# One set of PSUM banks for scores, turned probabilities and results in the soft-disc layer of a four-layer network, with four banks left to the side work, and an early start for that layer

## The chip, the cores and the metric

The program runs on one core of one Trainium2 chip, in one launch. The metric is the device time of an execution in microseconds (us). Everything is computed in fp32. A core has a matrix engine (TensorE, PE in the profile), a vector engine (VectorE, DVE), a scalar engine for functions such as Exp and Tanh (ScalarE, ACT), a general engine (GpSimd, POOL) and a queue that issues transfers (SyncE, SP). Matrix products land in PSUM, which the kernel uses as eight banks of 512 fp32 columns on 128 partitions. Each engine runs its instructions in the order in which they were written.

## The reference

The input has 8 images of 32x32 positions and 256 channels. Four layers follow each other, each of the form `x = x + f(groupnorm(x))`. Layer 0 is a retention layer, layer 1 a gated recurrent layer in its parallel form, layer 2 a 7x7 neighbourhood attention. The change touches layer 3, an attention with a soft disc as its window, 8 heads of 32 channels, cut here to what matters:

```python
qkv = silu(x @ w_qkv.T)                       # q, k, v
q, k = rms_norm(q, w_qn), rms_norm(k, w_kn)   # within each head
wp = silu(x @ w_wp.T + b_wp)                  # a width and a sharpness per head and position
...
k_win, v_win = unfold2d(k), unfold2d(v)       # 7 x 7 windows around each position
scores = einsum('blhd,blwhd->blhw', q, k_win) * D ** -0.5
soft_mask = sigmoid((width - rel_dist) * sharp)
attn = softmax(scores - (1 - soft_mask) * 10000)
out = einsum('blhw,blwhd->blhd', attn, v_win)
out = rms_norm(out, w_on)
return silu((out + v) @ w_out.T)
```

## The kernel before, in words

The layers run one after the other, and each hands its result to the next through device memory. `K.next` lets the last steps of a layer prepare the first image of the next one: a `First` object loads it, takes its statistics, loads the weights and normalises.

Layer 3 (`layer3`, class `DiscStream`) goes over the images in chunks. A chunk is one image and one half of the channels, that is four heads, so there are 16 chunks. In a chunk there are eight groups of 128 query positions (two 8x8 blocks) whose keys lie in 14x14 windows, 196 keys each. The main loop has a step `n` for each of the 128 groups, and each step works on several groups at once, at different stages:

- `scores(n + 3)`: 16 small matmuls (L1534) into four PSUM banks `s0` to `s3`, one for each head.
- `exps(n)`: Exp on ACT (L1557).
- `units(n)`: side work that is due (see below).
- `logits(n + 3)`: DVE reads the four score banks and adds the mask (L1547).
- `turn(n - 2, 0)`: four transposes on PE (L1575) put two heads' probabilities into one bank of the ring `m`, and one DVE copy of 112x512 (L1580) takes them to SBUF (`pts`).
- `finish()`: the second halves of the side work, which the units handed back.
- `soft(n + 5)` on ACT (L1963), `divide(n)` on DVE and POOL (L1564, L1565), `units(n + 0.5)`, `turn(n - 2, 1)` for the other two heads, and `finish()` again.
- `values(n - 3)`: 24 matmuls (L1591) into the bank `o`, and two DVE copies of 128x64 (L1599) to `oT`.
- `masked(n + 5)` on POOL (L1970).

The next step begins with its own `scores`. The order inside a step is written out by hand, and `manual_schedule` keeps it for PE, ACT, DVE and POOL. The framework puts in the waits: two engines' accesses to the same buffer wait for each other.

The side work is a list of units, each with a due time counted in steps (`Fillers`). It holds the projections of the next chunk (`project`: q, k and v in two halves each, one bank to a half, L1902; Tanh on ACT, L1887; the `rest` on DVE, L1912 and L1914; squares on POOL, L1922), the disc parameters (`discs`, L1935 to L1954), the root mean squares (`roots`, L1982 to L1998, with two changes of ACT's function table), `head_scale` (L2004, L2008), the values' strips and transposes (`in_strips` L2018, `vturn` L1608 and L1613), the group norm of the next image, and the tail of the image before (`tail_sq`, `tail_scale`, `output` L2050 to L2059). Each unit that uses PE takes a bank from the ring `m` and gives it back when its `rest` has read it.

PSUM in layer 3 is thus four score banks, three ring banks (shared by the units and the `pt` of `turn`) and one bank `o`.

Ahead of step 0 the loop begins at `n = -13`, where only units are due: chunk 0 is projected at -12 and on, the discs at -10, and so on. Before that, the head of `layer3` clears three padded key images (`kp`), the strips and nine probability tiles on POOL (L1830, L1518), and brings in the layer's constants by transfers issued from ACT's queue (L1834 to L1857), some of which DVE and POOL then scale (L1835, L1845 to L1850, L1855).

Of the kernel before, what the change touches and what calls it, by code (L numbers as in the profile page):

```python
# [16 lines left out]
P = 128  # L17
SIDE = 32
L = SIDE * SIDE
C = 256  # L20
# [137 lines left out]
class Base:  # L158
    def __init__(self, nc, pool, images, a):
        self.nc, self.pool, self.images = nc, pool, images  # L160
        idg = pool.tile([P, 2, P], F32, name="idg")
        nc.sync.dma_start(idg, a["k_id"])
        self.ident = idg[:, 0, :]
        self.g8 = idg[:, 1, :]
        self.mhalf = pool.tile([P, 2], F32, name="mhalf")
        nc.vector.memset(self.mhalf, -0.5)
        self.ring = None
        self.next = None

    def big(self, name):  # L170

# [183 lines left out]
class First3(First):  # L355
    def weights(self):

        nc = self.K.nc
        self.w = self.K.big("w3")[:, :, 0 : 768 + P]
        nc.vector.memset(self.w[:, :, 784:], 0.0)  # L360
        nc.sync.dma_start(self.w[:, :, 0:768], self.a["l3_qkv"])
        nc.sync.dma_start(self.w[:, :, 768:784], self.a["l3_wp"])

    def norm(self, c):
        if c == 0:
# [1137 lines left out]
class DiscStream(Stream):  # L1503
# [8 lines left out]
    def __init__(self, K, wk, cp, pp, pairs, n_img, ebufs):  # L1512
        super().__init__(K, wk, pp, pairs, n_img, ebufs)
        self.slots, self.s = 20, {}
        self.tiles = []
        for i in range(ebufs):
            t = cp.tile([P, 4, 2 * self.PART], F32, name=f"e{i}")
            self.nc.gpsimd.memset(t, 0.0)  # L1518
            self.tiles.append(t)

    def tile(self, n):
        return self.tiles[n % self.ebufs]
# [3 lines left out]

    def scores(self, n):
        b, c, t = self.groups[n]
        s = [self.pp.tile([P, HALF], F32, tag=f"s{j}", name=f"s{j}") for j in range(4)]
        q, k = self.q[b, c], self.k[b, c]  # L1530
        for g in range(2):
            for j in range(4):
                ch = slice(32 * j, 32 * j + 32)
                self.nc.tensor.matmul(  # L1534
                    grid(s[j][64 * g : 64 * g + 64, :NWIN], self.ROW),
                    q[ch, 64 * t.block(g) : 64 * t.block(g) + 64],
                    k[ch, t.krs[g] : t.krs[g] + self.ROW, t.kc : t.kc + self.ROW],
                    start=True, stop=True,
                )
        self.s[n] = s  # L1540
# [23 lines left out]
        self.nc.vector.reciprocal(self.su, self.su)  # L1564
        self.nc.gpsimd.tensor_mul(e, e, self.su.unsqueeze(2).to_broadcast([P, 4, NWIN]))  # L1565

    def turn(self, n, i):

        if i == 0:
            self.pts[n] = self.wk.tile([P, 2, HALF], F32, name="pts", bufs=2)  # L1570
        ps = self.ring("pt")
        for j in range(2):
            for k in range(2):
                at = (2 * j + k) * P
                self.nc.tensor.transpose(  # L1575
                    ps[: self.PART, at : at + P],
                    self.tile(n)[:, 2 * i + j, k * self.PART : (k + 1) * self.PART],
                    self.K.ident,
                )
        self.nc.vector.tensor_copy(self.pts[n][: self.PART, i, :], ps[: self.PART, :])  # L1580

    def values(self, n):
        b, c, t = self.groups[n]
        pts = self.pts.pop(n)
        v, at = self.v[b, c], 5 * t.col + t.rows[0]
        o = self.pp.tile([P, HALF], F32, tag="o", name="o")

        for k, q0, o0, w in ((1, 64, 0, P), (0, 0, 64, 64), (2, 192, 0, 64)):
            for j in range(4):
                p0 = (j % 2) * 2 * P + q0  # L1590
                self.nc.tensor.matmul(  # L1591
                    o[32 * j : 32 * j + 32, o0 : o0 + w],
                    v[: self.PART, at + k, 32 * j : 32 * j + 32],
                    pts[: self.PART, j // 2, p0 : p0 + w],
                    start=k == 1, stop=k != 1, skip_group_check=True,
                )
        for g in range(2):
            d = self.o[b, c][:, t.token(g) : t.token(g) + 1]
            self.nc.vector.tensor_copy(  # L1599
                bass.AP(d.tensor, d.offset, [d.ap[0], [SIDE, 8], [1, 8]]),  # L1600
                o[:, 64 - 64 * g : 128 - 64 * g].rearrange("p (i j) -> p i j", j=8),
            )
# [16 lines left out]
def layer2(tc, K, src, dst, n_img, a, first):  # L1619
# [3 lines left out]
    with tc.tile_pool(name="l2c", bufs=1, reuse_waits="tile") as cp, tc.tile_pool(  # L1623
# [132 lines left out]
        with tc.manual_schedule(engines={E.PE, E.Activation, E.DVE, E.Pool}):  # L1756
# [4 lines left out]
                    fill.add(at, lambda b=b: x.update({b: load(K.big("x"), b)}))  # L1761
            if K.next:
                nx, n = K.next, 16 * n_img
                fill.add(n - 22, nx.load)
                for i in range(4):
                    fill.add(n - 17 + i, lambda i=i: nx.stats(i))
                fill.add(n - 12, nx.mean)
                fill.add(n - 11, nx.root)
                fill.add(n - 7, nx.weights)
                for c in range(2):  # L1770
                    fill.add(n - 6 + c, lambda c=c: nx.norm(c))
# [42 lines left out]
def layer3(tc, K, src, dst, n_img, a, first):  # L1814
    nc = tc.nc
    pairs = disc_pairs()
    with tc.tile_pool(name="l3c", bufs=1, reuse_waits="tile") as cp, tc.tile_pool(
# [8 lines left out]
        xq[0], w = first.xq, first.w  # L1826
        kpad = [cp.tile([P, PADW, PADW], F32, name=f"kp{i}") for i in range(3)]
        strips = cp.tile([P, 4, PADW + 2, 14], F32, name="strips")
        for t in kpad + [strips]:
            nc.gpsimd.memset(t, 0.0)  # L1830
        st = DiscStream(K, wk, cp, pp, pairs, n_img, 9)
        K.ring = st.ring
        bwp = cp.tile([P, 16], F32, name="bwp")
        nc.scalar.dma_start(bwp, a["l3_bwp"].partition_broadcast(P))  # L1834
        nc.vector.tensor_scalar(bwp, bwp, 0.5, None, ALU.mult)  # L1835
        sel = cp.tile([P, 64], F32, name="sel3")
        nc.scalar.dma_start(sel, a["k_sel3"])
        spread = cp.tile([P, 2, P], F32, name="spread")
        nc.scalar.dma_start(spread[:, 0], a["k_spread"])
        nc.scalar.dma_start(spread[:, 1], a["k_spread"])  # L1840
        won = cp.tile([P, 2, P], F32, name="won")
        nc.scalar.dma_start(won.rearrange("p a b -> p (a b)"), a["l3_qkn"].partition_broadcast(P))


        nc.vector.tensor_mul(won[:, 0], won[:, 0], won[:, 1])  # L1845
        nc.vector.scalar_tensor_tensor(
            spread[:, 0], won[:, 0], -(32.0**-0.5) / MASK_SCALE, spread[:, 0],
            ALU.mult, ALU.mult,
        )
        nc.vector.memset(won, 0.0)  # L1850
        for h in range(2):
            nc.scalar.dma_start(won[32 * h + 8 : 32 * h + 9], a["l3_on"].unsqueeze(0))
        wo = cp.tile([P, 2, C], F32, name="wo3")
        nc.scalar.dma_start(wo, a["l3_out"])
        nc.gpsimd.tensor_scalar(wo, wo, 0.5, None, ALU.mult)  # L1855
        win = cp.tile([P, 2, NWIN], F32, name="win3")
        nc.scalar.dma_start(win, a["k_win3"])  # L1857
        eps = cp.tile([P, 1], F32, name="eps6")
        nc.vector.memset(eps, 1e-6)

        gn = first.gn

# [209 lines left out]
        def plan_chunk(J):  # L2072

            n, (b, c) = 8 * J, divmod(J, 2)
            for i in range(4):
# [7 lines left out]
        def plan_image(b):  # L2083
            n = 16 * b
            if b:
                fill.add(n - 27.5, lambda: load(b))
                for i in range(4):
                    fill.add(
                        n - 23.5 + i / 2,
                        lambda i=i: gn.stats(b, image_parts(x[b]), i),  # L2090
                    )
                fill.add(n - 21, lambda: gn.mean(b, later))
                fill.add(n - 19, lambda: gn.root(b, later))
                for c in range(2):
                    fill.add(n - 13.5 + c / 2, lambda c=c: normed(b, c))
            for u in range(2):
                fill.add(n - 10 + u / 2, lambda u=u: discs(b, u))
# [12 lines left out]
        for J in range(2 * n_img + 3):  # L2110
            b, c = divmod(J, 2)
            t = b - 2 if c == 0 and b >= 2 else None
            if J < 2 * n_img or t is not None:
# [18 lines left out]
        def finish():  # L2132
            while later:
                later.pop(0)()

        E = mybir.EngineType
        with tc.manual_schedule(engines={E.PE, E.Activation, E.DVE, E.Pool}):
            for n in range(-13, N + 3):
                if 0 <= n + 3 < N:
                    b, c, t = st.groups[n + 3]  # L2140
                    if t is pairs[0]:
# [6 lines left out]
                    st.logits(n + 3)  # L2148
                if 0 <= n - 2 < N:
                    st.turn(n - 2, 0)  # L2150
                finish()
                if 0 <= n + 5 < N:
                    soft(n + 5)
                if 0 <= n < N:
                    st.divide(n)
                units(n + 0.5)
                if 0 <= n - 2 < N:
                    st.turn(n - 2, 1)
                finish()
                if 0 <= n - 3 < N:  # L2160
                    st.values(n - 3)
                if 0 <= n + 5 < N:
                    masked(n + 5)
            for n in range(N + 3, N + 32):
                for h in (0, 0.5):
# [7 lines left out]
def body(tc, a, out, layers=LAYERS):  # L2173
# [7 lines left out]
    with tc.tile_pool(name="base", bufs=1) as bp, tc.tile_pool(name="images", bufs=1) as ip:  # L2181
# [10 lines left out]
        for i, layer in enumerate(layers):  # L2192
            K.next = first.get(i + 1)
            layer(tc, K, x[i], x[i + 1], n_img, a, first.get(i))


# [16 lines left out]
```

## Time and profile before

| | |
|---|---|
| median of 3 runs | 3490.29 us (3487.11 to 3499.76) |
| profiled execution | 3481.33 us, span 3479.5 us, mean granted TensorE clock 0.964 |
| busy share of the span | PE 94%, ACT 64%, DVE 62%, POOL 43% |
| layer 3 in the span | about 2622 to 3480 us |
| PE busy, 2700 to 2800 us | 86.40 of 100 us, granted clock 0.82 |
| PE busy, 3000 to 3100 and 3100 to 3200 us | 93.32 and 93.34 of 100 us, granted clock 0.95 and 0.97 |
| first scores of layer 3 | at 2660 us |

The busy shares cover the whole program, and each layer has limits of its own. For this change the stage is layer 3. The windows of that stage, its waits and the order of instructions in single steps are what is to be read; an engine's share in other layers says nothing on it.

### The profile page before, as it was taken

Reading aid. Unit: us, or ns where it says so; the run is one execution under the profiler, and the core shown is the slowest. Engines: PE = TensorE matmul, PEld = TensorE weight load, DVE = VectorE, ACT = ScalarE, POOL = GpSimd, SP = SyncE. Lnnn points to the kernel's source line nnn. Section 1 sums busy time; section 2 is a strip of 40 time slices with the busy share of each in tenths; the row PEclk is TensorE's granted clock in tenths of the full one; section 3 lists DMA queues with packets and bytes.
Section 4 is the critical chain, followed back from the end, with each engine's and each line's share of the span. In section 5 each row is a group of like instructions: output and inputs, shape, how many; then the busy total and the mean of one; then the engine's idle time right before and its main releaser. Section 6 shows DMA issues by size and latency. Waiting matters only on the chain.

```text
span 3479.5 us, 77392 instructions
## 1 busy us (share of the span) xinstructions
PE 3255.0 (94%) x30760; PEld 1655.6 (48%) x30760; DVE 2172.7 (62%) x5559; ACT 2237.1 (64%) x5022; POOL 1491.2 (43%) x1071
## 2 busy tenths in 40 slices
PE   7999999999998988899999989999998889999998
PEld 3323323323323444677676645555553545555454
DVE  4777677677675664555555545556564667677775
ACT  3667667667675554555555446666675778888885
POOL 4233233232221110345444443333335567777777
PEclk9999999999999998899999999999998889999999
DMA  3000000000003667577777531111111001101001
GB/s 135 13 25 1 25 25 1 25 25 1 25 25 116 236 199 256 162 199 179 203 210 187 136 112 38 38 38 50 50 48 43 2 14 38 32 29 35 26 26 59
DMA packets 139054, 268.44 MB, mean 77 GB/s; under 512 B 9218, under 2 KB 77188, under 8 KB 130372
## 3 DMA queue, kind: packets, MB, share of 16 engines
q1 hardware_dynamic: 131152, 241.90, 23.1%
q10 hardware_dynamic: 7540, 21.60, 1.9%
q8 instruction: 242, 3.96, 0.5%
q14 instruction: 120, 0.98, 0.1%
HBM read 178.27 MB, written 85.20 MB: 76 GB/s over the span
## 4 chain that ended last, share of the span: by engine, by line
PE 68%; ACT 10%; DVE 8%; DMA 5%; POOL 4%; issue 4%; SPq 0%; POOLq 0%; ACTq 0%; DVEq 0%
PE s L633 7%; PE sm L651 6%; PE num L678 5%; PE qkv_ps L1667 5%; PE qkv_ps L1902 4%; PE up_ps L808 3%; PE dn_ps L1205 3%; PE qk_ps L508 3%; DMA x<-x 3%; PE pt L1575 2%; PE pt L1447 2%; PE fac_ps L2004 2%; PE o_ps L561 2%; ACT e L1963 2%; DMA d<-l1rows 2%
## 5 line engine op out<-in xcount | busy, mean ns | idle before, releaser
L639 DVE TENSOR_TENSOR e<-s,ret 128x1024 f32<-128x1024 f32 x512 | 603.0, 1219 | 180.3 <-PE s L633 175.1
L643 ACT ACTIVATE ea<-e 128x1024 f32<-128x1024 f32 x512 | 535.9, 1056 | 267.0 <-DVE e L639 233.4
L633 PE MATMUL s<-qk,qk 32*128 32x512 f32 x2048 | 300.2, 640 | 2.6 <-POOL qk L525 1.9
L1580 DVE COPY pts<-pt 112x512 f32<-112x512 f32 x256 | 176.5, 690 | 181.0 <-PE pt L1575 179.1
L1433 POOL TENSOR_TENSOR e<-e,su 128x616 f32<-128x616 f32 (+2 forms) x128 | 157.4, 1230 | 287.0 <-DVE su L1432 278.8
L1013 POOL TENSOR_TENSOR d<-cmask,d 128x1024 f32<-128x1024 f32 x64 | 152.7, 2386 | 296.0 <-DMA d<-l1rows 183.5
L651 PE MATMUL sm<-ea,ones 128*32 128x512 f32 x2048 | 273.0, 604 | 2.0 <-DVE dn L659 2.0
L678 PE MATMUL num<-e,v 128*32 128x512 f32 x2048 | 266.6, 592 | 0.0
L808 PE MATMUL up_ps<-x,wup 128*128 128x512 f32 x512 | 233.5, 608 | 11.3 <-DVE gate L865 9.3
L1963 ACT ACTIVATE e<-win,disc 128x196 f32<-128x196 f32 x512 | 240.9, 548 | 0.2
L1565 POOL TENSOR_TENSOR e<-e,su 128x784 f32<-128x784 f32 x128 | 191.5, 1496 | 92.3 <-DVE su L1564 67.4
L1557 ACT ACTIVATE e<-e,mx 128x196 f32<-128x196 f32 x512 | 229.1, 456 | 0.0
L1970 POOL TENSOR_TENSOR e<-e,win 128x784 f32<-128x784 f32 x128 | 201.3, 1573 | 38.1 <-issue 32.9
L1667 PE MATMUL qkv_ps<-x,w 128*128 128x512 f32 x384 | 194.7, 644 | 21.3 <-POOL x L239 17.5
L1428 ACT ACTIVATE e<-e,mx 128x154 f32<-128x154 f32 (+2 forms) x512 | 213.4, 429 | 0.2 <-DVE mx L1416 0.2
L1902 PE MATMUL qkv_ps<-xq,w 128*128 128x512 f32 x384 | 199.5, 646 | 11.0 <-DVE kp L1914 5.4
L1575 PEld LDWEIGHTS pt<-idg,e 128*112 128x112 f32 x1024 | 121.1, 141 | 136.9 <-issue 60.1
L1575 PE MATMUL pt<-idg,e 128*112 128x128 f32 x1024 | 167.3, 290 | 19.2 <-DVE pts L1580 8.8
L633 PEld LDWEIGHTS s<-qk,qk 32*128 32x128 f32 x2048 | 85.1, 182 | 184.2 <-issue 121.5
L835 DVE SCALAR_TENSOR_TENSOR cv<-xm,par,cv 128x512 f32<-128x512 f32 x192 | 140.2, 750 | 48.8 <-ACT cv L830 46.2
L1022 ACT ACTIVATE d<-d,cols 128x128 f32<-128x128 f32 x512 | 164.1, 395 | 0.0
L1547 DVE CUSTOM_DVE_ANT_0 e<-s,e 128x196 f32<-128x196 f32 x512 | 154.0, 358 | 12.9 <-PE s L1534 7.8
(241 smaller groups left out, 6644.1 us busy)
## 6 DMA issues: line engine op xcount, KB each, us to landing
d<-l1rows SPq DMA_DIRECT2D x64, 512.0 KB
x<-x SPq DMA_DIRECT2D x25, 1024.0 KB
x<-x SPq DMA_DIRECT2D x32, 512.0 KB
l1xm<-xm SPq DMA_DIRECT2D x16, 1024.0 KB
l1sz<-sz SPq DMA_DIRECT2D x16, 1024.0 KB
xv<-l1xm SPq DMA_DIRECT2D x32, 512.0 KB
l1xa<-xa SPq DMA_DIRECT2D x16, 1024.0 KB
sz<-l1sz SPq DMA_DIRECT2D x16, 1024.0 KB
```

Source lines behind the costliest of these rows:

```text
L633: nc.tensor.matmul(s[:, j % 2], qk[b, 1, c][g, kb * P : (kb + 1) * P], qk[b, 0, c][g, h * HALF : (h + 1) * HALF], start=True, stop=True,)
L639: nc.vector.tensor_mul(e[n, i], s, m)
L643: nc.scalar.activation(ea[n, i], e[n, i], AF.Abs)
L651: nc.tensor.matmul(acc["sm"][g, :], ones, ea[n, j // 2][:, j % 2, :], start=kb == 0, stop=kb == 7,)
L678: nc.tensor.matmul(acc["num"][g, :], v[b][:, kb, vc], e[n, j // 2][:, j % 2, :], start=kb == 0, stop=kb == 7,)
L808: nc.tensor.matmul(ps, wup[:, kc, m * P : (m + 1) * P], seg(s)[:, kc], start=kc == 0, stop=kc == 1,)
L1428: self.nc.scalar.activation(p[:, j], p[:, j], AF.Exp, scale=-1.0, bias=mx[:, j : j + 1], accum_out=su[:, j : j + 1],)
L1557: self.nc.scalar.activation(e[:, j], e[:, j], AF.Exp, scale=-1.0, bias=mx[:, j : j + 1], accum_out=self.su[:, j : j + 1],)
L1575: self.nc.tensor.transpose(ps[: self.PART, at : at + P], self.tile(n)[:, 2 * i + j, k * self.PART : (k + 1) * self.PART], self.K.ident,)
L1667: nc.tensor.matmul(ps, w[:, kc, o : o + P], x[b][:, kc, h * HALF : (h + 1) * HALF], start=kc == 0, stop=kc == 1,)
L1902: nc.tensor.matmul(ps, w[:, kc, o : o + P], xq[b][:, kc, h * HALF : (h + 1) * HALF], start=kc == 0, stop=kc == 1,)
L1963: nc.scalar.activation(e[:, j], win[:, 0], AF.Tanh, scale=disc[b][:, i, 8 + h : 9 + h], bias=disc[b][:, i, h : h + 1],)
```

## The change

It has three parts. First, PSUM: layer 3 now has four tiles `b0` to `b3`, one bank each, cut into two halves of 256 columns. The first half of each takes the scores of one head. The second half of `b0` takes the results `o`; the second halves of `b1`, `b2`, `b3` take the turned probabilities, one head at a time in rotation (`turns`). The ring `m` has four banks, for the units alone. `turn` now handles one head: two transposes and one copy of 112x256, called four times in a step.

Second, the constants: they are loaded and scaled during layer 2 (`First3.early`, three units at steps 88, 92 and 96 of 128), by transfers of the SP queue, into a pool `late` that lives from layer 1 to layer 3.

Third, the first chunk: the loop's steps -13 to -5 are replaced by `start()`, which writes the work of chunk 0 out in an order of its own. Only one padded key image, the strips and three probability tiles are cleared ahead of it, and the others at its end. The statistics of image 1 move to steps -3 and later, and the discs of image 0 go through `start()` alone.

```diff
+    def early(self):
+        nc, a, pool = self.K.nc, self.a, self.K.late
+        def loads():
+            self.bwp = pool.tile([P, 16], F32, name="bwp")
+            nc.sync.dma_start(self.bwp, a["l3_bwp"].partition_broadcast(P))
...
+        def factors():
+            won, spread = self.won, self.spread
+            nc.vector.tensor_scalar(self.bwp, self.bwp, 0.5, None, ALU.mult)
+            nc.gpsimd.tensor_scalar(self.wo, self.wo, 0.5, None, ALU.mult)
...
+        def weight():
+            for h in range(2):
+                nc.sync.dma_start(
+                    self.won[32 * h + 8 : 32 * h + 9], a["l3_on"].unsqueeze(0)
+                )
+        return [loads, factors, weight]
...
+        self.tiles = [cp.tile(shape, F32, name=f"e{i}") for i in range(ebufs)]
+        self.banks = [pp.tile([P, 2, HALF // 2], F32, name=f"b{j}") for j in range(4)]
+        self.turns = 0
+    def ring(self, name):
+        return self.pp.tile([P, HALF], F32, tag="m", name=name, bufs=4)
...
-        s = [self.pp.tile([P, HALF], F32, tag=f"s{j}", name=f"s{j}") for j in range(4)]
+        s = [self.banks[j][:, 0] for j in range(4)]
...
-    def turn(self, n, i):
-        if i == 0:
+    def turn(self, n, j):
+        if j == 0:
             self.pts[n] = self.wk.tile([P, 2, HALF], F32, name="pts", bufs=2)
-        ps = self.ring("pt")
...
-        self.nc.vector.tensor_copy(self.pts[n][: self.PART, i, :], ps[: self.PART, :])
+        ps = self.banks[1 + self.turns % 3][:, 1]
+        self.turns += 1
+        for k in range(2):
+            self.nc.tensor.transpose(
+                ps[: self.PART, k * P : k * P + P],
+                self.tile(n)[:, j, k * self.PART : (k + 1) * self.PART],
+                self.K.ident,
+            )
+        at = (j % 2) * 2 * P
+        self.nc.vector.tensor_copy(
+            self.pts[n][: self.PART, j // 2, at : at + 2 * P], ps[: self.PART]
+        )
     def values(self, n):
...
-        o = self.pp.tile([P, HALF], F32, tag="o", name="o")
+        o = self.banks[0][:, 1]
...
+                for i, u in enumerate(nx.early()):
+                    fill.add(n - 40 + 4 * i, u)
...
-        bwp = cp.tile([P, 16], F32, name="bwp")
-        nc.scalar.dma_start(bwp, a["l3_bwp"].partition_broadcast(P))
...
+        def start():
+            units(-11)
+            rest = [discs(0, 0), discs(0, 1), project(0, 1, 0)]
+            rest[0]()
+            rest[2]()
+            r = project(0, 1, 1)
+            rest[1]()
+            r()
+            soft(0)
+            for h in range(2):
+                project(0, 0, h)()
+            soft(1)
+            rest = [project(0, 2, h) for h in range(2)]
+            for f in rest:
+                f()
+            masked(0)
+            roots(0, None)
+            in_strips(0)
+            for i in range(4):
+                head_scale(0, 1 - i // 2, i % 2)()
+            masked(1)
+            for i in range(3, 9):
+                st.clear(i)
+            for t in kpad[1:]:
+                nc.gpsimd.memset(t, 0.0)
...
-            for n in range(-13, N + 3):
+            start()
+            for n in range(-4, N + 3):
...
                     st.turn(n - 2, 0)
+                    st.turn(n - 2, 1)
...
-                    st.turn(n - 2, 1)
+                    st.turn(n - 2, 2)
+                    st.turn(n - 2, 3)
```

More of the change, by code (lines that the diff above doesn't have):

```diff
@@ L168, in __init__ @@
         self.next = None
+        self.late = pool
     def big(self, name):
@@ L362, in weights @@
         nc.sync.dma_start(self.w[:, :, 768:784], self.a["l3_wp"])
+    def early(self):
[3 more added lines that the diff above has]
+            nc.sync.dma_start(self.bwp, a["l3_bwp"].partition_broadcast(P))
+            self.sel = pool.tile([P, 64], F32, name="sel3")
+            nc.sync.dma_start(self.sel, a["k_sel3"])
+            self.spread = pool.tile([P, 2, P], F32, name="spread")
+            nc.sync.dma_start(self.spread[:, 0], a["k_spread"])
+            nc.sync.dma_start(self.spread[:, 1], a["k_spread"])
+            self.won = pool.tile([P, 2, P], F32, name="won")
+            nc.sync.dma_start(
+                self.won.rearrange("p a b -> p (a b)"), a["l3_qkn"].partition_broadcast(P)
+            )
+            self.wo = pool.tile([P, 2, C], F32, name="wo3")
+            nc.sync.dma_start(self.wo, a["l3_out"])
+            self.win = pool.tile([P, 2, NWIN], F32, name="win3")
+            nc.sync.dma_start(self.win, a["k_win3"])
+            self.eps = pool.tile([P, 1], F32, name="eps6")
+            nc.vector.memset(self.eps, 1e-6)
+        def factors():
+            won, spread = self.won, self.spread
+            nc.vector.tensor_scalar(self.bwp, self.bwp, 0.5, None, ALU.mult)
+            nc.gpsimd.tensor_scalar(self.wo, self.wo, 0.5, None, ALU.mult)
+            nc.vector.tensor_mul(won[:, 0], won[:, 0], won[:, 1])
+            nc.vector.scalar_tensor_tensor(
+                spread[:, 0], won[:, 0], -(32.0**-0.5) / MASK_SCALE, spread[:, 0],
+                ALU.mult, ALU.mult,
+            )
+            nc.vector.memset(won, 0.0)
+        def weight():
+            for h in range(2):
+                nc.sync.dma_start(
+                    self.won[32 * h + 8 : 32 * h + 9], a["l3_on"].unsqueeze(0)
+                )
+        return [loads, factors, weight]
     def norm(self, c):
@@ L1514, in __init__, with clear @@
         self.slots, self.s = 20, {}
[L1515 to L1519, printed above, removed]
+        shape = [P, 4, 2 * self.PART]
+        self.tiles = [cp.tile(shape, F32, name=f"e{i}") for i in range(ebufs)]
[3 more added lines that the diff above has]
+        return self.pp.tile([P, HALF], F32, tag="m", name=name, bufs=4)
+    def clear(self, i):
+        self.nc.gpsimd.memset(self.tiles[i], 0.0)
     def tile(self, n):
@@ L1565, in divide @@
         self.nc.gpsimd.tensor_mul(e, e, self.su.unsqueeze(2).to_broadcast([P, 4, NWIN]))
-    def turn(self, n, i):
-        if i == 0:
+    def turn(self, n, j):
+        if j == 0:
             self.pts[n] = self.wk.tile([P, 2, HALF], F32, name="pts", bufs=2)
-        ps = self.ring("pt")
[L1572 to L1580, printed above, removed]
+        ps = self.banks[1 + self.turns % 3][:, 1]
[5 more added lines that the diff above has]
+                self.K.ident,
+            )
+        at = (j % 2) * 2 * P
+        self.nc.vector.tensor_copy(
+            self.pts[n][: self.PART, j // 2, at : at + 2 * P], ps[: self.PART]
+        )
     def values(self, n):
@@ L1828, in layer3 @@
         strips = cp.tile([P, 4, PADW + 2, 14], F32, name="strips")
-        for t in kpad + [strips]:
+        for t in (kpad[0], strips):
             nc.gpsimd.memset(t, 0.0)
         st = DiscStream(K, wk, cp, pp, pairs, n_img, 9)
+        for i in range(3):
+            st.clear(i)
         K.ring = st.ring
-        bwp = cp.tile([P, 16], F32, name="bwp")
-        nc.scalar.dma_start(bwp, a["l3_bwp"].partition_broadcast(P))
[L1835 to L1859, printed above, removed]
+        bwp, sel, spread, won = first.bwp, first.sel, first.spread, first.won
+        wo, win, eps = first.wo, first.win, first.eps
         gn = first.gn
@@ L2074, in plan_chunk @@
             n, (b, c) = 8 * J, divmod(J, 2)
+            if J == 0:
+                return
             for i in range(4):
@@ L2088, in plan_image @@
                     fill.add(
-                        n - 23.5 + i / 2,
+                        max(n - 23.5, -3) + i / 2,
                         lambda i=i: gn.stats(b, image_parts(x[b]), i),
                     )
-                fill.add(n - 21, lambda: gn.mean(b, later))
-                fill.add(n - 19, lambda: gn.root(b, later))
+                fill.add(max(n - 21, -1), lambda: gn.mean(b, later))
+                fill.add(max(n - 19, 1), lambda: gn.root(b, later))
                 for c in range(2):
                     fill.add(n - 13.5 + c / 2, lambda c=c: normed(b, c))
-            for u in range(2):
-                fill.add(n - 10 + u / 2, lambda u=u: discs(b, u))
+                for u in range(2):
+                    fill.add(n - 10 + u / 2, lambda u=u: discs(b, u))
             for c in range(2):
@@ L2112, in layer3 @@
             t = b - 2 if c == 0 and b >= 2 else None
-            if J < 2 * n_img or t is not None:
+            if J and (J < 2 * n_img or t is not None):
                 fill.add(8 * J - 8, lambda J=J, t=t: roots(J, t))
@@ L2134, in finish @@
                 later.pop(0)()
+        def start():
[20 more added lines that the diff above has]
+            for i in range(3, 9):
+                st.clear(i)
+            for t in kpad[1:]:
+                nc.gpsimd.memset(t, 0.0)
         E = mybir.EngineType
         with tc.manual_schedule(engines={E.PE, E.Activation, E.DVE, E.Pool}):
[L2138 removed]
+            start()
+            for n in range(-4, N + 3):
                 if 0 <= n + 3 < N:
@@ L2150, in layer3 @@
                     st.turn(n - 2, 0)
+                    st.turn(n - 2, 1)
                 finish()
-                if 0 <= n + 5 < N:
+                if 1 < n + 5 < N:
                     soft(n + 5)
@@ L2161, in layer3 @@
                     st.values(n - 3)
-                if 0 <= n + 5 < N:
+                if 1 < n + 5 < N:
                     masked(n + 5)
@@ L2191, in body @@
                 first[0].alone()
-        for i, layer in enumerate(layers):
-            K.next = first.get(i + 1)
-            layer(tc, K, x[i], x[i + 1], n_img, a, first.get(i))
+        K.next = first.get(1)
+        layers[0](tc, K, x[0], x[1], n_img, a, first.get(0))
+        with tc.tile_pool(name="late", bufs=1) as K.late:
+            for i, layer in enumerate(layers[1:], 1):
+                K.next = first.get(i + 1)
+                layer(tc, K, x[i], x[i + 1], n_img, a, first[i])
 def kernel(**inputs):
```

## The prediction

> **What bounds the kernel now.** I read the page first (busy shares, chain of waits), then the windows of layer 3, PE's waits there, and single steps in the timeline.
>
> The windows give for each stretch of 100 us the busy time of PE, PEld, DVE, ACT and POOL, then the granted clock:
>
> ```profile
> 2700.00:2800.00 100.00, 86.40 (x871) 48.13 (x869) 60.82 (x244) 76.82 (x219) 59.47 (x44) 0.82 0.01 1
> 3000.00:3100.00 100.00, 93.32 (x955) 51.10 (x955) 68.86 (x262) 80.87 (x229) 73.19 (x55) 0.95 0.10 31
> 3100.00:3200.00 100.00, 93.34 (x959) 50.38 (x958) 70.54 (x275) 82.44 (x237) 74.92 (x57) 0.97 0.12 34
> ```
>
> Layer 3 is bound by PE; 100 us is about one image, 16 steps of 6.3 us, with 6.7 us of PE idle. From 2700 to 3400 us PE idles 13.6, 8.8, 5.7, 6.7, 6.7, 6.7 and 4.4 us, 52.6 in all. What ended the idle time between 3000 and 3200 us is in PE's waits (total, times, longest):
>
> ```profile
> PE out_ps L2050 <- ACT v L1613: 4.0, 2, 2.0
> PE out_ps L2050 <- ACT e L1557: 1.9, 2, 0.9
> PE vt L1608 <- DVE pts L1580: 1.6, 2, 0.8
> PE fac_ps L2004 <- DVE pts L1580: 1.6, 2, 0.8
> PE qkv_ps L1902 <- DVE pts L1580: 1.6, 2, 0.8
> ```
>
> These five are 10.7 of 13.3 us: a unit waits for a bank of the shared ring, held by `pt` until its copy or by a unit until ACT reads it. That is what four banks of their own would remove.
>
> Now the end of one step in the timeline (start, duration, engine, line; the order of writing is kept on each engine):
>
> ```profile
> 3070.67 0.65 PE L1591 MATMUL o<-pts,v 112*32 112x128 f32 x24
> 3071.25 0.59 PE L1534 MATMUL s<-kp,qT 32*64 32x196 f32 x16
> 3070.78 0.69 DVE L1580 COPY pts<-pt 112x512 f32<-112x512 f32 x1 [1.76 <-PE pt L1575]
> 3071.38 0.68 DVE L1912 SCALAR_TENSOR_TENSOR qT<-th,qkv_ps 128x512 f32<-128x512 f32 x1
> 3071.98 0.35 DVE L1599 COPY oT<-o 128x64 f32<-128x64 f32 x2
> 3072.24 0.35 DVE L1547 CUSTOM_DVE_ANT_0 e<-s,e 128x196 f32<-128x196 f32 x1
> ```
>
> PE goes from the results (L1591) straight to the next step's scores (L1534). DVE takes the results only 0.7 us later, since the copy of `pts` and a unit's `rest` stand ahead of it in its queue. That costs nothing today, because `o` and the scores lie in different banks.
>
> **Part 1, the shared banks: a new wait in every step.** In the change `o` is the second half of `b0`, and the first matmul of the next scores writes the first half of `b0`. If two engines are kept apart by bank, the scores wait until both copies of `o` have ended, and behind the scores waits all of PE's queue: the units, the turns, the next values. For the 121 steps that the rows tell apart (of 125) I took the end of L1599 less the start of the following L1534, that is, how far PE now runs ahead. The smallest is 0.49 us. There are 20 under 0.8 us (12.3 us together), 75 between 0.97 and 1.16 (81.8) and 26 from 1.6 to 5.4 (87.3), in all 181 us. A handover of this kind already shows in the trace once, where the drain of layer 2 has nothing between two results in one bank:
>
> ```profile
> 2613.67 0.29 DVE L1474 COPY oT<-o 128x128 f32<-128x128 f32 x1
> 2614.11 0.61 PE L1466 MATMUL o<-pts,v 77*32 77x64 f32 x29 [0.50 <-DVE oT L1474]
> ```
>
> PE stood 0.50 us there, which agrees with the 0.49. So the bounds of the price are 125 x 0.49 = 61 us and 181 us. Between them I go by kind of step. The usual step (75) has the copy of `pts` ahead: two copies of 256 columns replace one of 512, the first starts two transposes earlier, and the second takes 0.41 us by the 121x256 copy of layer 2 (L1451) against 0.69, so 1.08 becomes 0.80: 60 us. The 20 short ones keep 0.55: 11. In the 26 long ones DVE waits for ACT: a `rest` wants its Tanh behind `soft`, behind the table loads of `roots`, or in the chain of a disc. PE comes later by about 0.8 in each step before them, and ACT, busy 81%, uses that to catch up; only the disc's chain of some 3 us (3119 to 3121 and 3122 to 3125 us) is inherent. I take 1.8 each: 47. Together 118 us.
>
> The Trainium skill has a rule on this, in "PSUM — Partial Sum Buffer", section "PSUM bank collisions raise a hardware error": PE and DVE may not touch one bank in the same 32 partitions at once, whether or not the columns differ, and software must guard by bank, not by address. The row above shows only waits on the same columns. By the page the 118 us are due; without its rule they would be nil.
>
> A second wait of the same kind: the turns write into `b1` to `b3` and so wait for `logits` of the same step. From the end of the scores to the first transposes there are 1.5 us or more in most steps, and logits take about 1.2 (four times 0.28). In about five steps of 16 only 0.93 to 0.98 us lie between, so some 0.3 us each, 13 us; in the others units cover it. Bounds 0 and 125 x 0.3 = 38; I take 10, near the low end, since units stand there in most steps.
>
> DVE's work grows: 512 copies at about 0.41 us, pipelined some 0.33 apart, against 256 at 0.69 (0.60 apart): 15 us, beside PE, which DVE at 70% hides, apart from what is counted above. The transposes stay the same in number.
>
> **Four banks for the units.** They can give back at most the 52.6 us of idle. I take 40, because the waits for `pts` and for ACT's `v` are of that kind and the first image's idle is partly ACT's.
>
> **Part 2, constants.** Their nine transfers leave ACT's queue and go through SP's during layer 2, where SP issues few; 0.5 us each on SP, nothing on the path. DVE gets about 1 us and POOL one 1.49 us operation (L1855) inside layer 2. PE is 95% busy there and waits for POOL's division, so 0 to 2.5 us; I take 1.5. What they free is seen in the chain:
>
> ```profile
> 2622.64 5.34 DMA x<-xr
> 2628.01 3.74 DMA won<-l_qkn
> 2631.77 0.30 DVE won L1845
> ...
> 2660.23 0.52 PE s L1534 x16
> ```
>
> ACT's queue stops at `won`, whose memory the last store of layer 2 holds until 2628; ACT's first Tanh runs at 2630.7 though the product was there at 2624.6.
>
> **Part 3, the start.** Before, the scores begin 37.6 us after the last DVE work of layer 2 (2622.6). After: PE needs 4.2 (discs) + 7.5 (k, q) + 3.7 (v) = 15.4 us without the stall, to 2638; then Tanh of v 1.2, table load 1.28, Ln and Exp 1.3, first root factor and its multiplication 1.2 and 0.6 for each of three more: 2645; two projections of chunk 1 partly beside it, some 2.5: 2647.5. That is 12.5 us earlier. Least: only ACT's 6 us; most: 20, if the projections hide wholly and POOL's clearing (7.4 us now behind `masked(1)`, ahead of the squares of chunk 1) costs nothing.
>
> **Clock.** After a 10 us window with PE busy 6.66 (2670 to 2680) the granted clock falls to 0.50 for some 20 us, and at 3150 to 3160 it is 0.67 after a window with 8.67. More idle time may bring more of it: one more such stretch an image is 3.3 us, 26 in all. I take 10, bounds 0 and 26.
>
> The skill's "TensorE: Matmul & The Clock Gate", section "What's actually happening", lets the clock fall after an idle window of about 3.4 us. The stretch at 3150 has no idle piece that long before it, so row and page differ here; by the page the term would be 0, by the row 10.
>
> **Sum** against the profiled execution (span 3479.5, time 3481.33): +118 +10 +1.5 +10 -40 -12.5 = +87, 3568 us. That execution lies 9 us under the median of the runs, so I add the 87 to the median: 3577 us.
>
> **Rivals.**
> *The relief outweighs the handover (faster or equal).* Place: the same end of a step. For it: PE's idle is nearly all ring waits, and the two copies alone take 0.35 us. At 0.35 the wait is 44 us, and 44 - 52.6 - 12.5 = -21: 3469 us. It decides from a mean handover below (52.6 + 12.5) / 125 = 0.52 us. Against it: the smallest of the 121 gaps is 0.49, and 75 of them hold a copy and a `rest` ahead.
> *The full gap is paid.* If ACT does not catch up, 181 + 10 + 26 + 1.5 - 20 - 12.5 = +186: 3676 us. Against it: ACT has 18% to spare.
> *The halves do not wait for each other*, the change not being what it seems: -40 - 12.5 + 1.5 = -51: 3439 us. Against it: the row at 2614 shows that waits by buffer are put in, and `b0` is one buffer.
>
> **How the numbers follow.** Forecast 0.69, relief 0.17, full gap 0.09, no wait 0.05. A measurement here can tell about 0.5% (17 us) from no change. Faster by more: all of no wait and 0.10 of the relief, 0.15; within: 0.07 of the relief and 0.01 of the forecast, 0.08; slower: 0.77. The range leaves out most of the no wait, some of the relief and the upper full gap: 3470 to 3660.
>
> **What would show it.** Right: ahead of L1534 PE idles 0.5 to 1 us in each step, released by DVE `oT` (L1599's copy); PE busy falls to some 84 to 88 per 100 us and an image takes about 112 us; ring waits for `pts` are gone; the first scores start some 25 us after layer 2's last DVE work instead of 38. Wrong: no idle ahead of the scores, PE busy of 97 or more, or layer 3 shorter than 845 us.

## The result and the profile after

The changed kernel takes 3677.91 us (median of 4 runs, 3676.97 to 3684.7) against 3493.23 for the kernel before: a ratio of 1.0533, 95% interval 1.0508 to 1.0557, so 5.3% slower. The direction was forecast; 3577 us and the range up to 3660 were too low. The span of the profiled execution is 3675.4 us, 195.8 more than before.

The windows of layer 3 (busy time of PE, PEld, DVE, ACT, POOL, then the granted clock), for the same stretches as before:

```profile
2700.00:2800.00 100.00, 79.34 (x847) 46.42 (x845) 61.75 (x261) 71.42 (x205) 55.24 (x42) 0.86 0.01 1
3000.00:3100.00 100.00, 84.11 (x783) 46.34 (x784) 57.79 (x236) 62.42 (x177) 60.81 (x46) 0.85 0.06 20
3100.00:3200.00 100.00, 83.58 (x753) 42.66 (x748) 60.18 (x247) 65.69 (x186) 61.98 (x46) 0.86 0.10 30
```

Two things are worse at once: PE is busy 84 us of 100 and not 93, and its clock is 0.85 and not 0.95. Every other engine is less busy than before, so none of them is short of time. PE's waits from 3000 to 3224 us are down to two:

```profile
PE b L1587 <- DVE oT L1654: 35.3, 29, 3.3
PE b L1627 <- DVE mx L1600: 2.1, 6, 0.5
```

No unit waits for a bank any more. The scores (L1587) wait for the copies of the results (L1654), 29 times. The timeline of the after kernel has an ordinary handover (the copies of `pts`, a `rest`, the copies of `oT`, and then the scores):

```profile
3114.97 0.76 DVE L1633 COPY pts<-b 112x256 f32<-112x256 f32 x2 [0.51 <-PE b L1627]
3115.09 0.65 PE L1646 MATMUL b<-pts,v 112*32 112x128 f32 x24
3115.65 0.68 DVE L2091 SCALAR_TENSOR_TENSOR th<-th,out_ps 128x512 f32<-128x512 f32 x1
3116.24 0.35 DVE L1654 COPY oT<-b 128x64 f32<-128x64 f32 x2
3116.64 0.60 PE L1587 MATMUL b<-kp,qT 32*64 32x196 f32 x16 [0.91 <-DVE oT L1654]
```

and a long one, where the `rest` waits for a Tanh that stands behind a table load and `soft`:

```profile
3102.40 1.88 PE L1936 MATMUL qkv_ps<-xq,w 128*128 128x512 f32 x4
3103.38 1.28 ACT L1997 ACT_TABLE_LOAD   x1
3104.64 0.65 PE L1646 MATMUL b<-pts,v 112*32 112x128 f32 x24
3104.68 1.88 ACT L1997 ACTIVATE e<-win,disc 128x196 f32<-128x196 f32 x4
3106.45 0.57 ACT L1921 ACTIVATE th<-qkv_ps 128x512 f32<-128x512 f32 x1
3107.06 0.75 DVE L1948 SCALAR_TENSOR_TENSOR vT<-th,qkv_ps 128x256 f32<-128x256 f32 x2 [1.77 <-ACT th L1921]
3107.73 0.35 DVE L1654 COPY oT<-b 128x64 f32<-128x64 f32 x2
3108.13 0.96 PE L1587 MATMUL b<-kp,qT 32*64 32x196 f32 x16 [2.84 <-DVE oT L1654]
3109.03 3.10 PE L1936 MATMUL qkv_ps<-xq,w 128*128 128x512 f32 x4
```

The last row is what follows such a wait: four matmuls of a projection, which took 1.88 us in the first row, take 3.10. On the pages the projections show it as a mean, 646 ns before (first line) and 717 after, with the same number of instructions:

```profile
L1902 PE MATMUL qkv_ps<-xq,w 128*128 128x512 f32 x384 | 199.5, 646 | 11.0 <-DVE kp L1914 5.4
L1936 PE MATMUL qkv_ps<-xq,w 128*128 128x512 f32 x384 | 224.1, 717 | 0.8 <-DVE kp L2042 0.8
```

For the account I cut the trace at the first and the last scores of layer 3. Before, this stretch is 769.6 us long, PE busy in 708.4 and idle in 61.2, of which 5.2 ahead of the scores. After, it is 967.5 long, busy 808.8, idle 158.7, of which 143.4 ahead of the scores. So of the 195.8 us of span, 97.5 are PE's idle time, 100.4 are PE's longer busy time with the same work, -13.5 the earlier first scores, 8.8 lie ahead of layer 3 and 2.6 behind the last scores.

### The profile page after: what moved, and what is told of

It is laid out like the page before. It is cut to its first block, busy times and chain, and to the rows that moved or that the text cites. A ratio compares the mean times of both kernels' runs of the same rounds, so it can differ in the third digit from the quotient of the medians.

```text
span 3675.4 us, 77623 instructions
## 1 busy us (share of the span) xinstructions
PE 3352.5 (91%) x30760; PEld 1702.0 (46%) x30760; DVE 2209.1 (60%) x5815; ACT 2233.2 (61%) x5022; POOL 1491.3 (41%) x1071
## 4 chain that ended last, share of the span: by engine, by line
PE 68%; DVE 10%; ACT 8%; DMA 6%; POOL 4%; issue 3%; SPq 0%; POOLq 0%; ACTq 0%; DVEq 0%
PE s L679 7%; PE sm L697 6%; PE num L724 5%; PE qkv_ps L1936 5%; PE qkv_ps L1722 5%; PE b L1627 3%; DMA x<-x 3%; PE up_ps L854 3%; PE qk_ps L554 3%; PE dn_ps L1251 3%; PE b L1587 2%; PE pt L1493 2%; DMA d<-l1rows 2%; PE fac_ps L2038 2%; DVE pts L1633 2%
## 5 line engine op out<-in xcount | busy, mean ns | idle before, releaser
L1633 DVE COPY pts<-b 112x256 f32<-112x256 f32 x512 | 199.7, 420 | 256.4 <-PE b L1627 255.6
L1587 PE MATMUL b<-kp,qT 32*64 32x196 f32 x2048 | 95.5, 425 | 143.4 <-DVE oT L1654 139.5
L1936 PE MATMUL qkv_ps<-xq,w 128*128 128x512 f32 x384 | 224.1, 717 | 0.8 <-DVE kp L2042 0.8
L1600 DVE CUSTOM_DVE_ANT_0 e<-b,e 128x196 f32<-128x196 f32 x512 | 154.9, 358 | 106.6 <-PE b L1587 106.5
L1627 PEld LDWEIGHTS b<-idg,e 128*112 128x112 f32 x1024 | 138.6, 156 | 154.5 <-issue 102.5
L1627 PE MATMUL b<-idg,e 128*112 128x128 f32 x1024 | 189.9, 318 | 17.1 <-DVE mx L1600 15.7
L1921 ACT ACTIVATE th<-qkv_ps 128x512 f32<-128x512 f32 x96 | 56.3, 589 | 219.6 <-PE qkv_ps L1936 217.9
```

The lines of the kernel that those rows point to most:

```text
L1627: self.nc.tensor.transpose(ps[: self.PART, k * P : k * P + P], self.tile(n)[:, j, k * self.PART : (k + 1) * self.PART], self.K.ident,)
L1633: self.nc.vector.tensor_copy(self.pts[n][: self.PART, j // 2, at : at + 2 * P], ps[: self.PART])
L1936: nc.tensor.matmul(ps, w[:, kc, o : o + P], xq[b][:, kc, h * HALF : (h + 1) * HALF], start=kc == 0, stop=kc == 1,)
```

## The experiments

The theory after the result: the handover of `o` makes PE idle in each step (first half of the loss), and this idle time lowers PE's granted clock (second half). Rivals: that turned probabilities in the score banks cost as much as `o`; that the new start or the early constants lose time; that PE is slower for shared banks as such.

All kernels in one table. "Idle" is PE's between the first and the last scores, "at scores" the part ahead of the scores' matmuls, "half clock" the time of that stretch in which the trace's clock record has 0.5. The kernel before had medians of 3486.7 to 3487.3 us beside the experiments, and 3493.23 beside the changed kernel.

| kernel | median us | ratio, 95% interval | idle us | at scores | half clock us |
|---|---|---|---|---|---|
| before | 3487 | | 61 | 5 | 109 |
| after | 3677.91 | 1.0533 (1.0508 to 1.0557) | 159 | 143 | 358 |
| e1_start | 3487.88 | 1.0000 (0.9988 to 1.0011) | 59 | 2 | 140 |
| e2_psum_alone | 3687.85 | 1.0578 (1.0561 to 1.0594) | 159 | 144 | 373 |
| e3_o_alone | 3510.57 | 1.0064 (1.0041 to 1.0088) | 69 | 2 | 143 |
| e4_o_shared | 3691.76 | 1.0578 (1.0560 to 1.0596) | 167 | 167 | 389 |
| e5_ring3 | 3686.59 | 1.0578 (1.0559 to 1.0598) | 157 | 139 | 399 |
| e6_dummy | 3594.54 | 1.0309 (1.0294 to 1.0324) | 65 | 43 | 82 |
| e12_half_dummy | 3605.65 | 1.0337 (1.0323 to 1.0351) | 99 | 76 | 143 |
| e8_values_early | 3564.16 | 1.0214 (1.0192 to 1.0236) | 46 | 11 | 164 |
| e9_o_early_ring4 | 3465.21 | 0.9944 (0.9928 to 0.9961) | 45 | 9 | 102 |
| e10_order_alone | 3477.36 | 0.9959 (0.9940 to 0.9977) | 37 | 5 | 133 |
| e11_o_mid_ring4 | 3457.35 | 0.9920 (0.9900 to 0.9939) | 40 | 20 | 108 |

The three columns on the right come from one profiled execution of each kernel, e9's 15 us below its median and e5's 11 above. e1, equal in time, has 31 us more at half clock than the kernel before, so differences of that size in a single profile say little.

### Which part

**e1_start**: the change without its PSUM part.

```diff
-        self.banks = [pp.tile([P, 2, HALF // 2], F32, name=f"b{j}") for j in range(4)]
-        return self.pp.tile([P, HALF], F32, tag="m", name=name, bufs=4)
+        return self.pp.tile([P, HALF], F32, tag="m", name=name, bufs=3)
...   (scores, turn, values as before)
```

> The constants and the start as in the change, PSUM as before (four score banks, a ring of three with pt, o alone). By the theory that the whole loss is the shared banks, this is faster than before by the 13 us by which the first scores came earlier in the changed kernel: about 3480 us, with PE's idle time between the first and last scores unchanged at about 61 us. The rival, that the new start or the transfers in layer 2 bring part of the loss (layer 2 ended 9 us later in the changed kernel's trace), expects 3490 to 3500 us or more.

No difference in time. In its profile the first scores stand 27.0 us after layer 2's last DVE work, 10.5 earlier than before, but the stretch to the last scores is 779.9 us and not 769.6, with 31 us more at half clock. So neither expectation held as put: the other two parts bring no loss, and the gain of the start was given back behind it in that profile.

**e2_psum_alone**: the PSUM part put into the kernel before.

> The shared score banks and the units' four banks put into the kernel before, with its constants and its start unchanged. Theory: the whole loss is here, since e1_start (the other two parts) gave no difference: 3670 to 3700 us. Rival, the parts act together (the start's order makes the handover worse): 3600 to 3650 us.

3687.85 us: the whole loss, with idle time and half clock as in the changed kernel.

### Which of the shared halves

**e3_o_alone**: `o` in a bank of its own, a ring of three.

```diff
-        o = self.banks[0][:, 1]
+        o = self.pp.tile([P, HALF], F32, tag="o", name="o")
-        return self.pp.tile([P, HALF], F32, tag="m", name=name, bufs=4)
+        return self.pp.tile([P, HALF], F32, tag="m", name=name, bufs=3)
```

> The change, but o has a bank of its own again and the units a ring of three; the turned probabilities stay in the second halves of the score banks b1 to b3. Theory of the handover: the wait of the scores for the copies of o goes, and what is left is the wait for the last turn's copy, which stands ahead of the rests in DVE's queue, and ends at about the end of the values: PE's idle between first and last scores falls from 159 to 40 to 70 us, the clock comes back, 3470 to 3500 us. Rival, any sharing of a score bank costs as much: the scores then wait for pts instead, idle stays over 120 us and the time over 3600 us.

The wait at the scores is gone, and with it 167 us of 3678. It stays 0.6% over the kernel before, 10 us above what I expected. PE's waits from 2900 to 3400 us in e3 are one line,

```profile
PE b L1627 <- DVE mx L1600: 31.6, 27, 2.4
```

the transposes waiting for the logits of the bank that they share, the second wait of the prediction. The kernel before has waits of 28.8 us in the same stretch, all but 0.3 of them for ring banks. The units' own banks took one wait away and the shared banks brought another of about the same size, so this alone doesn't make the 0.6%. Against e1, which has as much time at half clock and differs from e3 only in where the turned probabilities go, e3 has 10 us more of PE's idle time between the first and the last scores, and its score matmuls are busy for 86.8 us and not 77.3. They hide a wait of some 0.1 us a step: in the rows below the last turn's copies end at 3144.99, and the group of score matmuls, which starts at 3144.92 and takes 0.70 us (0.59 in e1), has a matmul starting at 3145.04.

```profile
3144.23 0.76 DVE L1633 COPY pts<-b 112x256 f32<-112x256 f32 x2 [0.74 <-PE b L1627]
3144.92 0.70 PE L1587 MATMUL b<-kp,qT 32*64 32x196 f32 x16
```

**e4_o_shared**: only `o` shares a bank with scores; the turned probabilities go through the ring of four, two heads at a time.

> The change, but the turned probabilities go through the ring of four again, two heads at a time, and only o shares a bank with scores. Theory of the handover: nothing of the loss goes, 3640 to 3700 us, idle ahead of the scores of some 140 us and more because the copy of 512 columns stands ahead of the results again. Rival, the turned probabilities in the score banks are the cost: 3480 to 3550 us.

3691.76 us, nothing gained. So the loss is `o`'s. In this order of work the turned probabilities in the score banks cost about the 0.6% of e3; with the values early they cost more (e8 below).

### Whether the clock is caused by the waiting

**e5_ring3** and **e6_dummy**. The first frees a bank (`bufs=3`). The second fills PE's wait with a product that nobody reads:

```diff
                 if 0 <= n - 3 < N:
                     st.values(n - 3)
+                    nc.tensor.matmul(st.spare, w[:, 0, 0:P], w[:, 1, 0:HALF], start=True, stop=True)
```

> The change with three unit banks instead of four, so that one bank is free. Theory of the handover: PE waits for no unit's bank in the changed kernel, so the fourth bank is worth next to nothing there: 3678 us, give or take 15. Rival, the fourth bank has been hiding part of the loss: 3700 us or more. This is also the kernel that e6_dummy is to be compared with.

> As e5_ring3, and PE multiplies one 128x512 product of weights into the free bank behind the values of each step, which nobody reads (0.95 us at the full clock, 125 times, 119 us of extra work). Theory of the clock: PE's idle time at the handover, 143 us ahead of the scores, makes the granted clock fall, which costs PE some 115 us more than before; with the wait filled the clock comes back and the kernel is FASTER with the extra work in it, 3570 to 3630 us, with the half-clock time between first and last scores under 200 us instead of 358. Rival, the longer PE time has another cause (the banks shared): no gain, 3680 to 3740 us, half-clock time still over 300 us.

e5 is 3686.59 us, so the fourth bank is worth little there. e6 does 128 products more (134 us of PE time between its first and last scores) and is 92 us faster than e5. The windows from 3000 to 3100 us, e5 first:

```profile
3000.00:3100.00 100.00, 85.63 (x732) 45.54 (x731) 55.91 (x232) 56.20 (x162) 56.74 (x42) 0.79 0.06 17
```

and e6:

```profile
3000.00:3100.00 100.00, 93.24 (x841) 47.78 (x840) 62.73 (x254) 71.03 (x199) 60.42 (x45) 0.95 0.10 33
```

The banks are shared in both, so sharing as such is not what keeps PE slow. The idle time lowers the clock.

**e12_half_dummy**: the same with 256 columns.

> As e6_dummy with half the idle time filled: one product of 128x256 behind the values of each step (about 0.47 us at the full clock). Theory of the clock: half-clock time between first and last scores lies between the 399 us of e5_ring3 and the 82 us of e6_dummy, and the time below the 3687 us of e5_ring3, at 3590 to 3650 us. Rival, it is all or nothing and half the filling leaves the clock low: 3680 us or more.

3605.65 us and 143 us of half clock. Half the filling brings most of the clock back: 256 of the 317 us that e6 brings.

### Whether the order at the step's end matters

**e8_values_early**: the change, with the values ahead of the second half step's units.

```diff
+                if 0 <= n - 3 < N:
+                    st.values(n - 3)
                 units(n + 0.5)
                 if 0 <= n - 2 < N:
                     st.turn(n - 2, 2)
                     st.turn(n - 2, 3)
                 finish()
-                if 0 <= n - 3 < N:
-                    st.values(n - 3)
```

> The change with all its banks, but the values stand ahead of the second half step's units and turns instead of at the step's end, so that DVE takes the results while PE does those units and turns. Theory of the handover: the scores then wait only for the last turn's copy (about 0.4 us after the last transposes, 128 times, 50 us in all, against 140), and some of the clock comes back: 3500 to 3580 us. Rival, that the order at the step's end does not matter and PE is slow for sharing banks as such: 3660 us or more.

3564.16 us: 114 us of the loss go by order alone. The wait that is left shows as busy time and not as idle time, inside the group of 16 score matmuls:

```profile
3106.51 0.76 DVE L1633 COPY pts<-b 112x256 f32<-112x256 f32 x2 [0.97 <-PE b L1627]
3106.62 0.55 PE L1587 MATMUL b<-kp,qT 32*64 32x196 f32 x2
3107.32 0.59 PE L1587 MATMUL b<-kp,qT 32*64 32x196 f32 x14
```

and, where it does not split the row, as `3100.70 1.27` for 16 matmuls that take 0.59. Between the first and the last scores this group is 153.5 us busy in e8 and 77.0 before: 76 us, or 0.6 in each step and not the 0.4 expected. Nearly all of it is waiting for the last turn's copy in one of `b1` to `b3` (above, the copies end at 3107.27 and the third matmul starts at 3107.32; in more than half of the groups the last matmul ends 0.63 to 0.65 us after the last copy), which the values had covered when they stood at the end; e1, with about as much time at half clock as e8, has 77.3.

**e9_o_early_ring4**: `o` in the first score bank, values early, and the turned probabilities in the ring, now of four. **e10_order_alone**: the kernel before with the values early.

> The constants and the start of the change; o in the second half of the first score bank; turned probabilities through the ring, two heads at a time, as before, the ring now of four banks; and the values ahead of the second half step's units. Theory: with the values early the copies of o end long before the next scores, so the shared bank costs nothing, and a ring of four removes most of the 59 us that PE waits with a ring of three: idle between first and last scores 15 to 35 us, half-clock time at most that of before (109 to 140 us), 3430 to 3465 us, faster than both kernels. Rival, units wait for ACT and not for banks, so that a fourth bank moves the wait elsewhere: 3480 to 3500 us.

> The kernel before with the values ahead of the second half step's units and nothing else changed. Theory: order alone is worth nothing where o has a bank of its own, 3480 to 3500 us, idle about 60 us. Rival, the order itself is what helps e9_o_early_ring4 (DVE gets the results out of its way): 3450 to 3475 us.

e9 is faster than both kernels, 3465.21 us, at the upper end of what I expected; its idle time is 45 us and not 15 to 35. e10 says that the order is worth part of it with nothing shared, 0.4%, which I had not expected: 3477.36 us lies between the theory (3480 and more) and its rival (3475 and less), so both missed. In e9 PE still waits 23.4 us from 2900 to 3400 for the logits of the bank that takes `o`.

**e11_o_mid_ring4**: as e9, the values between the second half step's units and its turn.

```diff
                 units(n + 0.5)
+                if 0 <= n - 3 < N:
+                    st.values(n - 3)
                 if 0 <= n - 2 < N:
                     st.turn(n - 2, 1)
```

> As e9_o_early_ring4, but the values stand between the second half step's units and its turns. In e9 PE waited 23 us in 500 for the logits of the bank that takes o, since only two transposes' bank stood between; here the units stand between too. Theory: that wait goes, the scores still find the copies of o ended, because a turn stands between: idle 15 to 30 us instead of 45, 3435 to 3460 us. Rival, the copies of o come too late again behind a rest of the first half step: idle ahead of the scores of 40 us or more, 3470 to 3500 us.

3457.35 us, 0.8% under the kernel before, the lowest median of all, though its interval overlaps that of e9. Its waits from 2900 to 3400 us:

```profile
PE b L1587 <- DVE oT L1652: 8.3, 16, 1.0
PE vt L1661 <- ACT v L1666: 4.6, 5, 0.9
PE b L1644 <- DVE mx L1600: 4.2, 4, 1.6
```

17 us against 28.8 before. Idle between first and last scores was 40 and not the 15 to 30 expected; more than half of it lies ahead of 2900 us, where the window from 2700 to 2800 has PE busy 88.47.

## Why the prediction was wrong

**The handover was right, in kind and nearly in size.** Forecast 118 us; the idle time ahead of the scores rose by 138 (5.2 to 143.4). The 101 waits up to 1.6 us average 0.77 (0.80 was taken). The 22 longer ones average 3.0 and not the 1.8 that was taken for 26. Seven of them are the disc's chain, 3.3 each, which the prediction had seen as inherent. In 14 others the Tanh of v stands at the end of a chain on ACT (Ln, Exp, table load, `soft`), as in the long handover above. ACT did not catch up there: in eight of the 14 it had itself been idle for 1.0 to 1.6 us ahead of the Ln, so what held the Tanh was the chain and not a backlog.

**Second wait and ring relief.** 10 and -40 were taken; together PE's other idle time went from 56.0 to 15.3, -41. The transposes' wait for logits is 15.7 us on the whole page. So PE's idle time rose by 97.5 us where the sum had 118 + 10 - 40 = 88: luck in part, since the handover was 20 us too low and the other two terms together 11 too high.

**The clock was the step that failed.** The mechanism was named in the prediction, but its term was mis-sized: 10 us, bounds 0 and 26, by one more stretch at half clock in each image. Measured: time at half clock 109 to 358 us, and weighed with PE's busy time (half of it lost) 52.7 to 167.4, so 115 us; PE's busy time rose by 100.4. With the 100 in place of the 10 the sum passes the upper end of the range. e6 shows that this is the idle time's doing. A row that would have given the size was in the first fence of the prediction: 2700 to 2800 us, PE idle 13.6%, clock 0.82. The forecast itself had PE busy at 84 to 88%, and did not put that row's clock on it. An estimate from it: 0.18 of some 860 us of layer 3 (769.6 + 88) is 155, less the 55 lost already (half of 109), so 100 us. It gives a size and not a rule, since the changed kernel has 0.86 in the same window with PE only 79.34 busy. An image took about 121 us (967.5 for eight) and not the 112 that the prediction named as a sign.

**The skill's rules.** The rule to guard by bank, in "PSUM — Partial Sum Buffer", section "PSUM bank collisions raise a hardware error", pointed the right way where the rows were silent: `o` and scores, on different columns of `b0`, did wait for each other. But the framework puts this wait in. No run shows what would happen without it, or whether it goes by the bank or by the tile `b0`, which is one bank here. "TensorE: Matmul & The Clock Gate", section "What's actually happening", has the clock fall after an idle window of about 3.4 us. Read as a rule on single idle pieces, it makes the term nil. The longest idle piece of PE between the first and last scores is 3.7 us, there is one over 3.31, and the waits at the scores average 1.15 us a step, yet the clock was at half for 358 of 967 us; the measurement decides.

**Start and constants.** The first scores came 13.5 us earlier (12.5 forecast), yet e1 gives no time for it. That the constants are free could not be settled: layer 2 ends between 2622.7 and 2634.0 us in the ten profiles with them, and between 2622.0 and 2623.2 in the three without. Most of the spread is in layer 1, where the pool `late` is opened but not used. I ran nothing that separates that.

**The rivals.** The rival of the full gap had the number, 3676, but not the mechanism: PE waits 143 us at the scores and not 181, and the rest is clock. The break-even of 0.52 us per handover stood: the mean was 1.15.

## What to carry to other kernels

Where two stages share a PSUM bank as `o` and the scores do here, the second one waits for the reader of the first, and behind it waits the whole queue; put other work of the writing engine between the two (e9, e11), or the reader's queue sets the pace. When a change adds idle time to a PE that was busy over 90%, price the clock as well, from a stretch of the same profile with as much idle time; here the clock doubled the loss. A wait inside a group of matmuls shows as busy time, so compare a group's busy time with its count as well as the idle column.

## What the runs showed of the hardware

The clock record changes in steps of 3.41 us. I cut the traces from 2700 to 3400 us into such windows and took PE's busy share in each. From full to half the clock went 10 times before, 28 after, 23 in e12 and 16 in e6, in 44 of these 77 cases behind a window less than half busy; of all 47 windows at full clock that were less than half busy, only three were not followed by a fall. The other 33 falls came behind busier windows (0.66 to 1.00). How long it stayed low differs more: the windows at half clock number 25, 77, 29 and 16. In these four traces it went back to full only behind windows that were at least 0.89 busy. In the changed kernel 24 of the 49 windows at half clock that were followed by another were 0.90 busy or less, most of them 0.86, against 2 of 15 before. So a wait in every step, short as it is, seems to help to keep the clock low once it has fallen. That half the filling brings most of the clock back (e12) agrees with it, but no run varied the share by itself.
